# Seven products in place of eight for the output projections of two graph-attention layers, attention of two batches in one go, and a group's norms on two engines

## Chip, cores and metric

The kernel runs on one core of a Trainium2 chip. The metric is the device time of the program in microseconds, 2984.36 us before the change (median of three runs, 2982.48 to 2985.09). The engines are named as in the profile: PE is TensorE (matrix products), PEld its weight loads, DVE is VectorE, ACT is ScalarE, POOL is GpSimd, and SP issues the DMA transfers.

## What is computed

There are 128 batches of 128 nodes with 512 features, in float32, and a mask of 128 x 128 for each batch. Two layers follow each other. Each is masked attention (4 heads of 64 in layer 0, 8 in layer 1), an output projection, the sum with the layer's input, and a norm over the 512 features:

```python
q, k, v = heads(x @ Wq), heads(x @ Wk), heads(x @ Wv)
sim = einsum('bhid,bhjd->bhij', q, k) * 64 ** -0.5
attn = softmax(where(mask, sim, neg))        # layer 1: mask | eye, and it norms x with gamma, beta before q, k, v
out = einsum('bhij,bhjd->bhid', attn, v)
x = layernorm(x + merge(out) @ Wo + bo)      # Wo: 256 x 512 in layer 0, 512 x 512 in layer 1
```

## The kernel before

Two batches form a group (`G = 2`), so there are 64 groups. The loop at the end runs `step(s)` for s = 0 to 66 (lines 591 to 600), with some work of the last batches after it. One step holds work of four groups, in a pipeline: the q, k, v products of layer 0 for group s (`product_0`, line 337), scores, masks and exponentials of layer 0 for group s - 1 and of layer 1 for group s - 3 (`scores`, line 386, for one batch of each at a time), the q and k products of layer 1 for group s - 2 and its v products one step later (`product`, line 275), and attention and output of the batches between (`attend`, line 458; `residual`, line 487). The scheduling is by hand: `step` issues everything in its order (lines 531 to 589), each engine works through its own instructions in that order, and semaphores hold an instruction back until its data are there and its buffer is free.

The q, k, v products already use a scheme of seven products instead of eight for a 2 x 2 block product (Strassen's, in Winograd's form). The two batches are the halves of the rows, the two halves of the inner dimension and of the columns are the other blocks. `sums` (line 257) makes four sums of input blocks on GpSimd, and `weight_sums` four of the weights once. The products are numbered 1 to 7 and are accumulated in three PSUM banks, which `INTO` (line 272) names: `a` takes 1, then 6, 7 and 4 on top, `f` takes 5 and then 3, `c` takes 2. Between two products of one bank the result so far is read out, by ScalarE for 1, 5, 6 and 4 and by VectorE, which adds two parts, for 2, 3 and 7.

The output projection doesn't use this scheme before the change. `attend` (line 458) multiplies probabilities and values of one batch, and ScalarE copies the result to `aT` (line 474). `residual` makes 2 (layer 0) or 4 (layer 1) products of 128 x 128 weights with 512 columns for one batch in one bank (line 493). VectorE adds the layer's input with the bias (line 499), takes mean and variance (lines 501, 503), GpSimd takes the roots (lines 506 to 517), and VectorE applies the norm (line 524). `addend` (line 476) adds the bias ahead of that, for layer 1 after ScalarE has multiplied with a ratio of roots (line 483), which stands in for a second norm of the input.

Other steps that are touched: `normalised` (line 427) takes the reciprocal of the exponentials' sums on VectorE and multiplies on GpSimd (line 433); `blocks` (line 436) turns blocks of 32 x 32 on VectorE and sends them to a scratch in HBM, and `probs_arrive` fetches them back as `pT`, transposed as a whole. The layers' inputs are transposed in the same way: `turn` (line 208), `arrive` (line 226), and then on ScalarE `in_order` for layer 0 (line 235) and `finish` with gamma and beta for layer 1 (line 245).

PSUM has eight banks: five rotate (`ps_mm`, line 44), and `a`, `f` and `a0` are fixed, with `f` shared by both layers.

Of the kernel before, what the change touches and what calls it, by code (L numbers as in the profile page):

```python
# [27 lines left out]
def kernel(ctx: ExitStack, tc: tile.TileContext, x, adj, wq, wk, wv, wo, bo,  # L28
# [13 lines left out]
    four = ctx.enter_context(tc.tile_pool(name="four", bufs=4))  # L42
    dram = ctx.enter_context(tc.tile_pool(name="dram", bufs=2, space=bass.MemoryType.DRAM))
    ps_mm = ctx.enter_context(tc.tile_pool(name="ps_mm", bufs=5, space=PSUM))
# [9 lines left out]
    later, waiting = [], []  # L54
# [5 lines left out]
    def exponentials(left=0):  # L60
        while len(waiting) > left:
            waiting.pop(0)()


    X, M = {}, {}

    def load(g):
        if g >= NG:
            return
        X[g] = four.tile([P, G, E], F32, tag="x", name=f"x_{g}")  # L70
        M[g] = four.tile([P, G, N], U8, tag="m", bufs=6, name=f"m_{g}")
        nc.sync.dma_start(X[g], x[g * G:(g + 1) * G].rearrange("b n e -> n b e"))
        nc.sync.dma_start(M[g], adj[g * G:(g + 1) * G].rearrange("b i j -> i b j"))
# [8 lines left out]
    mhalf = const.tile([P, 2], F32, name="mhalf")  # L82
# [25 lines left out]

    spare = []
    for tag, n in (("qk1", 4), ("v1", 2), ("xT1", 2), ("xs1", 2)):  # L110
        rows_n = one.tile([P, n, E], F32, tag=tag, name=f"raw_{tag}")
        spare.extend(rows_n[:, i] for i in range(n))

    def load_transposed(dst, src, name, scaled=0):
        rows, cols = src.shape
        raws = []
        for r in range(rows // P):
            if not spare:
                raw = three.tile([P, cols], F32, tag="h", bufs=7, name=f"{name}_{r}")
            else:  # L120
                raw = spare.pop(0)
            nc.sync.dma_start(raw, src[r * P:(r + 1) * P, :])
            raws.append(raw)
# [36 lines left out]
    def weight_sums():  # L160
        for w, ws in ((w1qk, wsqk), (w1v, wsv)):
            for c in range(KH):
                if w is w1qk:
                    b11, b12 = w[:, c, :, 0], w[:, c, :, 1]
                    b21, b22 = w[:, KH + c, :, 0], w[:, KH + c, :, 1]
                else:
                    b11, b12 = w[:, c, 0], w[:, c, 1]
                    b21, b22 = w[:, KH + c, 0], w[:, KH + c, 1]
                t2, t3, t4 = ws[:, 0, c], ws[:, 1, c], ws[:, 2, c]
                nc.vector.tensor_sub(t3, b22, b12)  # L170
                nc.vector.tensor_sub(b12, b12, b11)
                nc.vector.tensor_sub(t2, b22, b12)
                nc.vector.tensor_sub(t4, b21, t2)

    def weight_sums_0():
        b11, b12, b21, b22 = (w0[:, c:c + KH, h].rearrange("p c t f -> p c (t f)")
                              for c in (0, KH) for h in range(2))
        t2, t3, t4 = (ws0[:, i].rearrange("p c t f -> p c (t f)") for i in range(3))
# [4 lines left out]

    weight_sums_0()
    load_transposed(w1, w_qkv, "w_qkv", scaled=INNER[1])
    setup.append(turn_gamma_beta)
    load_transposed(wo1, w_out, "w_out")
    setup.append(weight_sums)

    WO = (wo0, wo1)  # L190
    RATIO, H, XT, QK, V, QKV = {}, {}, {}, {}, {}, {}
# [14 lines left out]
    TURNED, SCR, RAW = {}, {}, {}  # L206

    def turn(l, g, b):
        if not 0 <= g < NG:
            return  # L210
        if b == 0:
            TURNED[l] = one.tile([P, 4, G * KC * 32], F32, tag=f"turned{l}", name=f"turned{l}_{g}")
        src = X[g][:, b] if l == 0 else H[g, b]
        nc.vector.transpose(TURNED[l].rearrange("p a (b c i) -> p a b c i", b=G, c=KC)[:, :, b],
                            src.rearrange("p (c a i) -> p a c i", a=4, i=32))
        if b == G - 1:
            SCR[l] = put(TURNED[l], f"scr{l}_{g}")

    def arrive(l, g):
        if not 0 <= g < NG:  # L220
            return
        RAW[l] = one.tile([P, 4, G, KC, 32], F32, tag=f"raw{l}", name=f"raw{l}_{g}")
        fetch(RAW[l].rearrange("p a b c i -> p a (b c i)"), SCR[l])

    def first_transposed():
        xT = XT[0, 0] = one.tile([P, KC, T], F32, tag="xT0", name="xT0_0")
        for b in range(G):
            pt = mm_tile(f"xt_{b}")
            for c in range(KC):
                nc.tensor.transpose(pt[:, c * N:(c + 1) * N], X[0][:, b, c * P:(c + 1) * P], ident)  # L230
# [26 lines left out]
    def sums(l, g):  # L257
        xT = XT[l, g]
        xs = one.tile([P, 4, KH, N], F32, tag=f"xs{l}", name=f"xs{l}_{g}")
        a = xT.rearrange("p (h c) (b n) -> p b h c n", h=2, b=2)  # L260
# [6 lines left out]
        XS[l, g] = xs  # L267
# [69 lines left out]
    def product_0(g, *which):  # L337
# [5 lines left out]
        for i in which:  # L343
# [10 lines left out]
            elif first:  # L354
                tag = {"a": "a0", "f": "f"}[bank]
                ACC[0, bank] = ps_st.tile([P, 512], F32, tag=tag, name=f"{bank}0_{g}")
# [11 lines left out]
            if i in (1, 5, 6):  # L368
                e = one.tile([P, 512], F32, tag=("e5_0" if i == 5 else f"e{i}"), name=f"e0_{i}_{g}")
                EV[0, i] = e[:, :3 * P]  # L370
# [8 lines left out]
    SM, SUM, PT, AT, XB = {}, {}, {}, {}, {}  # L379
# [6 lines left out]
    def scores(k):  # L386
        both = members(k)
        made = []
        for l, g, b in both:
# [11 lines left out]
            made.append(ps)  # L401
        for (l, g, b), ps in zip(both, made):
            K = HEADS[l] // 2
            mask = M[g][:, b, :]
            if l == 1:
                m1 = two.tile([P, N], U8, tag="m1", name=f"m1_{g}_{b}")
                nc.vector.tensor_tensor(m1, mask, eye, op=ALU.max)
                mask = m1
# [8 lines left out]
            SM[l, g, b], SUM[l, g, b] = sm, total  # L417
            waiting.append(lambda sm=sm, nmax=nmax, total=total, K=K: exps(sm, nmax, total, K))
        exponentials(1)

    def exps(sm, nmax, total, K):
# [14 lines left out]
    def blocks(k):  # L436
# [6 lines left out]
        t = one.tile([P, 4, sum(HEADS), 32], F32, tag="turned", name=f"turned_{k}")  # L443
        pT = one.tile([P, 4, sum(HEADS), 32], F32, tag="pT", name=f"pT_{k}")
        for l, g, b in both:
            lo, hi = slots[l]
            sm = SM.pop((l, g, b)).rearrange("p s k (q r) -> p q (s k) r", r=32)
            nc.vector.transpose(t[:, :, lo:hi, :], sm)  # L448
            PT[l, g, b] = pT[:, :, lo:hi, :]
        lo, hi = slots[both[0][0]][0], slots[both[-1][0]][1]  # L450
        t, pT = (u[:, :, lo:hi, :].rearrange("p a h i -> p a (h i)") for u in (t, pT))
        SCR["p"] = pT, put(t, f"scrp{hi - lo}_{k}")
# [5 lines left out]
    def attend(k):  # L458
        both = members(k)
        if not both:  # L460
            return
        for l, g, b in both:
            K = HEADS[l] // 2
            pT = PT.pop((l, g, b))
            pm = mm_tile(f"av{l}_{g}_{b}")

            for h in range(HEADS[l]):
                s, kk = h % 2, h // 2
                o = pm[s * D:(s + 1) * D, kk * N:(kk + 1) * N]
                v = QKV[g][:, b, kk, 2, s * D:(s + 1) * D] if l == 0 else V[1, g][:, b, h * D:(h + 1) * D]  # L470
                nc.tensor.matmul(o.rearrange("p (a r) -> p a r", r=32), v, pT[:, :, s * K + kk, :],  # L471
                                 start=True, stop=True)
            AT[l, g, b] = two.tile([P, INNER[l]], F32, tag=f"aT{l}", name=f"aT{l}_{g}_{b}")
            nc.scalar.copy(AT[l, g, b], pm[:, :INNER[l]])  # L474

    def addend(l, k):

        for _, g, b in [m for m in members(k) if m[0] == l]:
            if l == 0:
                xin = X[g][:, b, :]  # L480
            else:
                xin = H.pop((g, b))
                nc.scalar.activation(xin, xin, AF.Copy, scale=RATIO.pop((g, b)))  # L483
            nc.gpsimd.tensor_tensor(xin, xin, (bias0, bias1)[l], op=ALU.add)  # L484
            XB[l, g, b] = xin

    def residual(l, k):
        for _, g, b in [m for m in members(k) if m[0] == l]:
            aT = AT.pop((l, g, b))
            nk = INNER[l] // P  # L490
            pm = mm_tile(f"o{l}_{g}_{b}")
            for c in range(nk):
                nc.tensor.matmul(pm, aT[:, c * P:(c + 1) * P], WO[l][:, c, :],  # L493
                                 start=(c == 0), stop=(c == nk - 1))
            if l == 0:
                y = three.tile([P, E], F32, tag="h", bufs=7, name=f"h_{g}_{b}")
            else:
                y = two.tile([P, E], F32, tag="y", name=f"y_{g}_{b}")
            nc.vector.tensor_add(y, pm, XB.pop((l, g, b)))
            st = three.tile([P, nc.vector.BN_STATS_DIM], F32, tag="st", name="st")  # L500
            nc.vector.bn_stats(st, y)
            mv = three.tile([P, nc.vector.BN_AGGR_DIM], F32, tag="mv", name=f"mv{l}_{g}_{b}")
            nc.vector.bn_aggr(mv, st)
            n = 2 - l
            ve = three.tile([P, 2], F32, tag="ve", name="ve")
            nc.gpsimd.tensor_scalar_add(ve[:, 0:1], mv[:, 1:2], EPS)  # L506
            if l == 0:


                nc.gpsimd.tensor_scalar(ve[:, 1:2], mv[:, 1:2], 1.0 + EPS, EPS * EPS,  # L510
                                        op0=ALU.mult, op1=ALU.add)
            r = three.tile([P, 2], F32, tag="rstd", name="rstd")
# [117 lines left out]
```

## Time and profile before

| | us |
|---|---|
| median of three runs | 2984.36 (2982.48 to 2985.09) |
| the profiled execution | 2984.46 |
| its span, first to last instruction | 2982.7 |
| TensorE busy | 2920.0 (98%) |
| VectorE busy | 1854.0 (62%) |
| GpSimd busy | 1567.4 (53%) |
| ScalarE busy | 1334.2 (45%) |
| output products, line 493, 1536 records | 713.2 |

The profile lists for each engine how long it was busy and, in the chain of work that ended last, which engine's work the end of the program was waiting for. A matmul in float32 appears as two records. The end of a matmul in the trace is modelled, and its duration reaches into the next matmul, so the difference of two starts is the better measure of what a group of matmuls takes. For a wait, the answer names the engine and line that ended last of all that were waited for.

### The profile page before, as it was taken

What the parts mean: (1) busy time and instruction counts of PE and PEld (TensorE: products, weight loads), DVE (VectorE), ACT (ScalarE), POOL (GpSimd) and SP (SyncE); (2) the same over time, 40 slices, a digit from 0 to 9 for tenths busy, and PEclk for the clock granted to TensorE, in tenths of its full rate; (3) what the DMA queues carried; (4) which work ended last, traced back from release to release, by engine and by line L of the source; (5) the groups of instructions that cost most, each with busy time, mean ns of one, the idle gap of its engine ahead of it and who ended that gap; (6) DMA issues with size and microseconds to landing.
All of it is one profiled execution on the core that took longest, in us unless ns stands there. A gap on an engine that the chain in (4) does not pass through costs nothing.

```text
span 2982.7 us, 59421 instructions
## 1 busy us (share of the span) xinstructions
PE 2920.0 (98%) x22089; PEld 2402.9 (81%) x22089; DVE 1854.0 (62%) x3291; ACT 1334.2 (45%) x4619; POOL 1567.4 (53%) x2055
## 2 busy tenths in 40 slices
PE   6899999999999999999999999999999999999997
PEld 5788888888888888888888888888888888888865
DVE  4466666666666666666656666666666666666654
ACT  2344444444444444444544444444444444444442
POOL 2455545545545555555555555455455455455543
PEclk8999999999999999999999999999999999999999
DMA  5454544544544544544544545545445445445332
GB/s 170 123 149 129 150 141 127 161 136 124 165 135 125 165 136 127 160 134 134 156 132 140 150 131 147 146 129 153 141 126 161 137 122 168 133 125 163 118 100 89
DMA packets 249136, 414.42 MB, mean 139 GB/s; under 512 B 41608, under 2 KB 181392, under 8 KB 248848
## 3 DMA queue, kind: packets, MB, share of 16 engines
q1 hardware_dynamic: 248848, 410.62, 46.3%
q8 instruction: 175, 2.87, 0.4%
q14 instruction: 113, 0.93, 0.1%
HBM read 209.72 MB, written 200.80 MB: 138 GB/s over the span
## 4 chain that ended last, share of the span: by engine, by line
PE 96%; DVE 1%; DMA 1%; ACT 1%; issue 0%; POOL 0%; SPq 0%; POOLq 0%; DVEq 0%; ACTq 0%
PE o L493 22%; PE qka L304 15%; PE a L361 12%; PE qkf L304 8%; PE va L304 8%; PE sc L400 6%; PE av L471 6%; PE f L361 6%; PE qkc L304 4%; PE vf L304 4%; PE c L361 3%; PE vc L304 2%; ACT sm L424 1%; DMA scrp<-turned 0%; DMA pT<-scrp 0%
## 5 line engine op out<-in xcount | busy, mean ns | idle before, releaser
L424 ACT ACTIVATE sm<-sm,nmax 128x128 f32<-128x128 f32 x1536 | 595.2, 389 | 618.6 <-DVE nmax L415 604.9
L493 PE MATMUL o<-wo,aT 128*128 128x512 f32 x1536 | 713.2, 600 | 10.0 <-ACT aT L474 10.0
L506 POOL TENSOR_SCALAR ve<-mv 128x1 f32<-128x1 f32 x256 | 57.0, 223 | 1133.0 <-DVE rec L432 798.8
L493 PEld LDWEIGHTS o<-wo,aT 128*128 128x128 f32 x1536 | 278.3, 191 | 269.3 <-issue 246.8
L433 POOL TENSOR_TENSOR sm<-sm,rec 128x512 f32<-128x512 f32 (+1 forms) x256 | 397.0, 1561 | 171.9 <-DVE rec L432 171.9
L412 DVE COPY_PREDICATED sm<-m,sc 128x512 f32<-128x512 uint8 (+1 forms) x512 | 271.0, 581 | 29.1 <-POOL sm L410 7.0
L424 ACT ACTIVATION_READ_ACCUMULATOR sm<-sm,nmax 128x1 f32 x1536 | 288.0, 187 | 0.0
L448 DVE STREAM_TRANSPOSE turned<-sm 128x512 f32<-128x512 f32 (+1 forms) x256 | 246.0, 965 | 45.0 <-POOL sm L433 45.0
L304 PE MATMUL qkf<-xs,w 128*128 128x128 f32 x2048 | 249.9, 275 | 0.1
L304 PE MATMUL qka<-xs,wsqk 128*128 128x128 f32 x2048 | 249.6, 275 | 0.0
L415 DVE TENSOR_REDUCE nmax<-sm 128x4 f32<-128x512 f32 (+1 forms) x256 | 244.0, 953 | 8.8
L304 PEld LDWEIGHTS qkf<-xs,w 128*128 128x128 f32 x2048 | 239.0, 192 | 0.6 <-POOL xs L266 0.4
L304 PEld LDWEIGHTS qka<-xs,wsqk 128*128 128x128 f32 x2048 | 239.0, 192 | 0.0
L524 DVE TENSOR_SCALAR h<-h,mv,rstd 128x512 f32<-128x512 f32 x128 | 70.0, 547 | 265.0 <-POOL rstd L513 265.0
L432 DVE RECIPROCAL rec<-total 128x4 f32<-128x4 f32 (+1 forms) x256 | 44.7, 175 | 296.6 <-ACT sm L424 296.6
L266 POOL TENSOR_TENSOR xs<-xT 128x256 f32<-128x256 f32 x256 | 186.0, 727 | 34.4 <-PE w_qkvt L129 14.5
L410 POOL MEMSET sm<- 128x512 f32 (+1 forms) x256 | 181.1, 735 | 1.4 <-DVE turned L448 1.3
L330 ACT COPY ev<-va 128x256 f32<-128x256 f32 x128 | 47.6, 372 | 298.7 <-PE va L304 298.7
L513 POOL TENSOR_TENSOR rstd<-ve,mhalf 128x2 f32<-128x2 f32 (+1 forms) x256 | 165.9, 648 | 21.3
L330 ACT COPY eqk<-qka 128x512 f32<-128x512 f32 x128 | 75.1, 587 | 214.4 <-PE qka L304 214.4
L484 POOL TENSOR_TENSOR h<-h,bias 128x512 f32<-128x512 f32 x128 | 162.7, 1271 | 7.0 <-ACT h L483 6.9
L484 POOL TENSOR_TENSOR x<-x,bias 128x512 f32<-128x512 f32 x128 | 162.2, 1267 | 0.0
(122 smaller groups left out, 5825.5 us busy)
## 6 DMA issues: line engine op xcount, KB each, us to landing
scrp<-turned SPq DMA_DIRECT2D x124, 768.0 KB, 3.3
pT<-scrp SPq DMA_DIRECT2D x496, 192.0 KB, 4.0
scr<-turned SPq DMA_DIRECT2D x127, 512.0 KB, 2.7
raw<-scr SPq DMA_DIRECT2D x508, 128.0 KB, 3.0
x<-in_x_dram SPq DMA_DIRECT2D x64, 512.0 KB, 4.2
out_dram<-y SPq DMA_DIRECT2D x128, 256.0 KB, 2.0
m<-in_adj_dram SPq DMA_DIRECT2D x64, 32.0 KB, 4.0
scrp<-turned SPq DMA_DIRECT2D x4, 512.0 KB, 3.2
```

Of the source, the lines that this page charges most:

```text
L266: nc.gpsimd.tensor_tensor(o, a0, a1, op=op)
L304: nc.tensor.matmul(o, lhsT, rhs, start=first and n == 0, stop=n == len(todo) - 1, skip_group_check=True)
L361: nc.tensor.matmul(acc[:, t * P:(t + 1) * P], lhsT, rhs, start=first and n == 0, stop=n == len(todo) - 1, skip_group_check=True)
L400: nc.tensor.matmul(ps[h % 2][:, h // 2, :], q_, k_, start=True, stop=True)
L410: nc.gpsimd.memset(sm, (NEG0, NEG1)[l])
L412: nc.vector.copy_predicated(sm[:, s], mask[:, None, :].to_broadcast([P, K, N]), ps[s][:, :K, :])
L415: nc.vector.tensor_reduce(nmax, sm, AX.X, ALU.max, negate=True)
L424: nc.scalar.activation(sm[:, s, k, :], sm[:, s, k, :], AF.Exp, bias=nmax[:, s, k:k + 1], accum_out=total[:, s, k:k + 1])
L433: nc.gpsimd.tensor_tensor(sm, sm, rec[:, :, :, None].to_broadcast([P, 2, K, N]), op=ALU.mult)
L448: nc.vector.transpose(t[:, :, lo:hi, :], sm)
L484: nc.gpsimd.tensor_tensor(xin, xin, (bias0, bias1)[l], op=ALU.add)
L493: nc.tensor.matmul(pm, aT[:, c * P:(c + 1) * P], WO[l][:, c, :], start=(c == 0), stop=(c == nk - 1))
```

## The change

Group rows are kept in one tile `R[g]`, and everything from input to output works in place in it: the bias is added to both batches at once, the output products are added part by part, and the norms are applied there. Six such tiles rotate.

- `attend(s)` now works on both batches of a group, for layer 0 of group s - 2 and layer 1 of group s - 4, once per step. In layer 0 both batches share one bank and one copy.
- `out_sums` makes the four sums of the attention outputs on GpSimd, and `weight_sums_out` those of the output weights, once. `out_product` makes the seven products, each of 256 columns. VectorE adds each bank's content to its part of `R[g]` after every product.
- PSUM: four rotating banks and `a`, `f`, `a0`, `f0`. The output products of layer 0 use `a` and `f`, those of layer 1 use `a0` and `f0`.
- `stats` and `roots` keep mean and roots of both batches together. In layer 0 the norm of batch 0 is VectorE's and that of batch 1 ScalarE's; in layer 1 both are ScalarE's, and both batches are stored by one transfer.
- The diagonal is put into both masks by one instruction (`with_self`).
- Both layers' transposed inputs share one buffer on the way out (`turned_in`) and one on the way back (`raw`).
- The order in `step` is written anew, and the loop runs one step further (s = 0 to 67) with nothing after it.

```diff
-    ps_mm = ctx.enter_context(tc.tile_pool(name="ps_mm", bufs=5, space=PSUM))
+    ps_mm = ctx.enter_context(tc.tile_pool(name="ps_mm", bufs=4, space=PSUM))
...
+    def out_product(l, g, *which):
...
+        aT, so = AT[l, g], SO[l, g]
+        hk = INNER[l] // P // 2
+        w, ws = WO[l], WSO[l]
+        EH = E // 2
+        for i in which:
+            left = {1: aT[:, 0, :hk], 2: aT[:, 0, hk:], 3: so[:, 3], 4: aT[:, 1, hk:], 5: so[:, 0],
+                    6: so[:, 1], 7: so[:, 2]}[i]
+            right = {1: w[:, :hk, :EH], 2: w[:, hk:, :EH], 3: w[:, hk:, EH:], 4: ws[:, 2],
+                     5: w[:, :hk, EH:], 6: ws[:, 0], 7: ws[:, 1]}[i]
+            bank, first = INTO[i]
...
+            acc = ACC["o", bank][:, :EH]
+            for c in range(hk):
+                nc.tensor.matmul(acc, left[:, c], right[:, c], start=first and c == 0, stop=c == hk - 1,
+                                 skip_group_check=True)
+            b, h = {1: (0, 0), 2: (0, 0), 6: (0, 1), 3: (0, 1), 5: (1, 1), 7: (1, 1), 4: (1, 0)}[i]
+            part = R[g][:, b, h * EH:(h + 1) * EH]
+            nc.vector.tensor_add(part, acc, part)
...
+    def out_sums(l, g):
...
+        so = SO[l, g] = one.tile([P, 4, K // 2, N], F32, tag=("so", "xs0")[l], name=f"so{l}_{g}")
+        halves_sums(so, AT[l, g].rearrange("p b (h c) n -> p b h c n", h=2))
...
+    def norms_0(g, mv, shift, root):
+
+        nc.vector.tensor_scalar(R[g][:, 0], R[g][:, 0], mv[:, 0, 0:1], root[:, 1, 0:1],
+                                op0=ALU.subtract, op1=ALU.mult)
+        nc.scalar.activation(R[g][:, 1], R[g][:, 1], AF.Identity, bias=shift[:, 1:2],
+                             scale=root[:, 1, 1:2])
+
+    def norms_1(g, shift, root):
+        for b in range(G):
+            nc.scalar.activation(R[g][:, b], R[g][:, b], AF.Identity, bias=shift[:, b:b + 1],
+                                 scale=root[:, 0, b:b + 1])
+        nc.sync.dma_start(out[g * G:(g + 1) * G].rearrange("b n e -> n b e"), R[g])
```

The order of a step after the change (`scores` only makes the products now; `masked` is the masking and the maximum, `exps` the exponentials):

```python
        k = 2 * s
        if s:
            load(s + 1)
        made = scores(k)
        masked(made, 0)
        masked(made, 1)
        exps(0, k)
        addend(0, s - 2)
        with_self(s - 2)
        p("qk", 4, g=s - 3)
        product_0(s, 1)
        attend(s)
        exps(1, k)
        out_sums(0, s - 2)
        product_0(s, 5)
        p("", g=-1)
        product_0(s, 2)
        p("", g=-1)
        out_product(0, s - 2, 1, 5, 2)
        normalised(k)
        addend(1, s - 4)
        out_product(0, s - 2, 6)
        product_0(s, 6)
        p("", g=-1)
        blocks(k, 0)
        out_product(0, s - 2, 3, 7)
        stats(0, s - 2, 0)
        product_0(s, 3)
        out_product(0, s - 2, 4)
        stats(0, s - 2, 1)
        p("v", 1, 5, g=s - 3)
        blocks(k, 1)
        p("v", 2, g=s - 3)
        flush()
        turn(1, s - 2)
        product_0(s, 7)
        arrive(1, s - 2)
        probs_arrive(k)
        k += 1
        made = scores(k)
        masked(made, 0)
        p("v", 6, g=s - 3)
        product_0(s, 4)
        exps(0, k)
        masked(made, 1)
        exps(1, k)
        p("v", 3, g=s - 3)
        out_sums(1, s - 4)
        out_product(1, s - 4, 1, 5, 2)
        p("v", 7, g=s - 3)
        out_product(1, s - 4, 6, 3)
        p("v", 4, g=s - 3)
        normalised(k)
        turn(0, s + 1)
        finish(s - 2)
        out_product(1, s - 4, 7)
        stats(1, s - 4, 0)
        blocks(k, 0, 1)
        arrive(0, s + 1)
        probs_arrive(k)
        p("qk", 1)
        p("qk", 5)
        out_product(1, s - 4, 4)
        stats(1, s - 4, 1)
        p("qk", 2)
        p("qk", 6)
        in_order(s + 1)
        flush()
        p("qk", 3, 7)
```

## The prediction, written before the result was known

> **What bounds the kernel now.** I read the page's busy shares first, then the chain that ended last, and then the TensorE timeline of one step in the middle of the run.
>
> ```profile
> PE 2920.0 (98%) x22089; PEld 2402.9 (81%) x22089; DVE 1854.0 (62%) x3291; ACT 1334.2 (45%) x4619; POOL 1567.4 (53%) x2055
> ...
> PE 96%; DVE 1%; DMA 1%; ACT 1%; issue 0%; POOL 0%; SPq 0%; POOLq 0%; DVEq 0%; ACTq 0%
> ```
>
> TensorE never rests and carries 96% of the chain. So a step is the sum of its matmuls, and every wait that TensorE gets is paid in full. In the timeline the columns are start, duration, engine, line, operation and count. Durations overlap the next group, so I read differences of starts.
>
> ```profile
> 1546.75 3.70 PE L493 MATMUL o<-wo,aT 128*128 128x512 f32 x8
> 1550.28 1.95 PE L304 MATMUL qka<-xT,wsqk 128*128 128x128 f32 x16
> 1552.16 0.66 PE L471 MATMUL av<-pT,qkv 128*64 128x128 f32 x8
> 1552.65 1.04 PE L471 MATMUL av<-pT,v 128*64 128x128 f32 x16
> 1553.62 1.16 PE L361 MATMUL a<-xT,w 128*128 128x128 f32 x8
> 1554.62 0.61 PE L361 MATMUL a<-w,xT 128*128 128x128 f32 x4
> ...
> 1560.56 1.88 PE L493 MATMUL o<-wo,aT 128*128 128x512 f32 x4
> 1562.28 1.03 PE L304 MATMUL va<-w,xT 128*128 128x256 f32 x4
> 1563.14 1.03 PE L304 MATMUL vf<-w,xs 128*128 128x256 f32 x4
> ...
> 1591.89 3.70 PE L493 MATMUL o<-wo,aT 128*128 128x512 f32 x8
> ```
>
> The step's period is 1591.89 - 1546.75 = 45.14 us, and 64 of them are 2889 us of the 2982.7 us span. Four records of 256 columns take 0.86 us (215 ns each), four of 512 take 1.72 us (430 each). Going into `av` or out of it costs about 0.1 us: sixteen 128-column records take 1.79 us elsewhere, 1.88 ahead of `av`; eight take 0.90, but 1.00 after it.
>
> What a wait costs is seen near the end of the run, where product 4 of `va` follows closely on VectorE's read of the same bank:
>
> ```profile
> 2878.06 0.41 DVE L335 TENSOR_TENSOR v<-va,ev 128x256 f32<-128x256 f32 x1
> 2878.53 1.13 PE L304 MATMUL va<-wsv,xT 128*128 128x256 f32 x4 [0.62 <-DVE v L335]
> 2879.59 0.66 PE L471 MATMUL av<-pT,qkv 128*64 128x128 f32 x8
> ```
>
> TensorE starts 0.06 us after VectorE's end, and those four records take 1.06 us where they take 0.96 in a steady step (1572.62 to 1573.58): 0.1 us more for the restart. A reader of PSUM starts 0.20 us after the next product's start (ACT's copy of `va`, 1563.34 against 1563.14). Last, ScalarE and GpSimd ahead of the large `qk` products of the middle step:
>
> ```profile
> 1575.11 0.35 ACT L332 COPY v<-va 128x256 f32<-128x256 f32 x1
> ...
> 1576.73 2.07 ACT L252 ACTIVATE xT<-raw,gb 128x256 f32<-128x256 f32 x4
> ```
>
> ```profile
> 1575.40 3.08 POOL L433 TENSOR_TENSOR sm<-sm,rec 128x512 f32<-128x512 f32 x2
> 1578.44 1.27 POOL L484 TENSOR_TENSOR h<-h,bias 128x512 f32<-128x512 f32 x1
> 1579.67 0.73 POOL L266 TENSOR_TENSOR xs<-xT 128x256 f32<-128x256 f32 x1
> ```
>
> Here `qk` 1 starts at 1579.54, after `xT` (done 1578.80), and `qk` 5 at 1581.33, after the first sum `xs` (done 1580.40). Both are ready in time by about 0.7 to 0.9 us. That is all the slack there is.
>
> **What the Trainium skill says.** "TensorE: Matmul & The Clock Gate", section "Back-to-back issue gap", gives N/2.4 + 2.5 ns for a warm matmul of N columns: 55.8, 109 and 216 ns for 128, 256 and 512. The trace has just twice that for a record (112, 215, 430 ns), so 256 columns are as cheap per column as 512. The same page, section "What's actually happening", lets the clock fall after an idle window of about 3.4 us. The trace agrees so far that the 0.62 us wait above slowed nothing lasting, so waits under 1 us are counted as waits alone. "PSUM — Partial Sum Buffer", section "PSUM bank collisions raise a hardware error", says that a bank is guarded as a whole against a write beside a read; the `va` lines show such a wait. "SBUF — State Buffer", section "Who interferes with whom", says that a two-port `tensor_scalar` on VectorE and GpSimd block each other. The norm of `y` (line 524), which stands beside GpSimd's work, takes 892 ns on average and that of `h` 547, which fits.
>
> **The change, part by part (per step of one group).**
>
> *Output products.* Removed: 24 records of 512 columns, 3.53 + 1.72 + 3.43 + 1.72 = 10.40 us, less 0.10 in the 3.53, which is the way out of `sc` and then falls to `qk` 4: 10.30. Added: seven products of 2 records (layer 0) and seven of 4 (layer 1), 42 x 0.2157 = 9.06 us. Gain 1.24 us.
>
> *Attention in one go.* One entry into the small tiles and one exit less: 0.19 us. Product 6 of layer 0 now waits 0.13 us for ScalarE's late copy of product 1 (a step's `a` takes 0.06 + 0.07 more than the others); in the new order that copy stands ahead of the attention copies. Together the step would be 45.14 - 1.24 - 0.19 - 0.13 = 43.58 us. There are ten more places where a product waits on another engine's result. By my walk they are met in time, output product 6 of layer 0 by only 0.1 us; I give back 0.1 (bounds 0 and 1.0, at none and at a restart of 0.1 each): 43.68.
>
> *Wait 1, a bank.* The new instruction order has output product 4 of layer 0, then `v` 1, both in bank `a`, with VectorE's add between. From product 4's end: 0.20 to the add; 0.08 as the add of `product_0` 3 stands ahead of it on VectorE (557 ns); 0.41 for 256 columns (line 335: 385 to 415); 0.05 to TensorE; 0.10 restart. 0.85 us (bounds 0.7 and 1.0), covered by nothing: all of TensorE's queue is behind `v` 1.
>
> *Wait 2, the transposed input.* `finish` now stands on ScalarE behind the copy of `v` 4, and only output product 7 (0.86 us) lies between `v` 4 and `qk` 1. From the end of `v` 4: 0.20, the copy 0.25 to the next start (1575.11 to 1575.36), the first part of `xT` 0.59, 0.05: `qk` 1 starts at 1.09 instead of 0.86. Its second matmul needs the next part, 0.50 later, and with 0.10 for the restart it ends at 1.59 + 1.56 + 0.10 = 3.25.
>
> *Wait 3, GpSimd.* `qk` 5 needs `sums` of layer 1, on GpSimd behind both `normalised` products, which need a reciprocal that VectorE reaches only after the add of output product 3 of layer 1. From that product's end (0.86 before the end of `v` 4): 0.20 + 0.33 (the add's start to the next) + 0.15 reciprocal + 0.09 + 3.04 (both `sm`) + 0.73 (first sum) + 0.05 = 4.59, that is 3.73 after `v` 4. TensorE is there at 3.25. Without waits it would have been at 0.86 + 1.79 = 2.65. Waits 2 and 3 together cost 3.73 - 2.65 + 0.10 = 1.18 us (bounds 0.6, if part of it is absorbed, and 1.8). Behind it wait all other `qk` products.
>
> *Other engines.* VectorE: four adds (2.73) and three norms (2.33) go, fourteen adds of 0.41 (5.74) come: 28.7 becomes about 29.4 us of a step. ScalarE gains three norms at 0.73 (line 483's price): 20.7 to 22.8. GpSimd gains the sums of the attention outputs, four at 0.73 and four of half that width (between 0.36 and 0.73, I take 0.45), and loses about 1 us of small roots: 24.5 to 28. All stay under 65%, so none is a bound by itself; only the places above count. The norm on ScalarE lets `turn` of layer 1 and behind it the add of `product_0` 7 go on VectorE some 22.7 us into the step; `product_0` 4, which needs that bank, is due at 23.7: covered by 1 us of `v` 6. Four rotating banks instead of five: the scores need all four at once, and the last reader, the add of `v` 2, ends 1 us earlier under `product_0` 7. The mask of both batches in one instruction, and the bias of both in one (about 2.5 us, twice line 484), cost VectorE and GpSimd nothing more. Output stores go from two of 256 KB to one of 512 KB; on SP they and the scratch transfers have about 5 us before attention needs them. The next input is fetched into a buffer shared with `finish`, behind the scratch of the attention blocks on SP; its reader comes some 8 us after `finish`. The load of `x` stands behind the store on SP; its reader is 30 us off.
>
> *Sum.* 43.68 + 0.85 + 1.18 = 45.71 us, 0.57 more than now; over 64 steps 36 us. At both ends: the last group's seven products are chained through one bank, with some 0.7 us for each of three adds, sums ahead of them, and one store twice as large: I take +5 us. In the first steps attention waits for its scratch transfer once a step and later than now (`av` waited 5.65 us for `pT` at 50.18 and 4.18 at 83.08): I take -5, so nothing for both together (bounds -10 and +15). 2984.46 + 36 = 3020. The profiled execution (2984.46) is 0.1 us from the median.
>
> **Rivals.**
> 1. *The gain arrives:* all three waits hidden, 43.68 x 64 instead of 45.14 x 64: 2984 - 93 = 2891. For it: 1.5 us of TensorE work really go. Against: waits 1 to 3 stand in the instruction order itself. Chance 0.07.
> 2. *GpSimd's and ScalarE's chain is shorter than its parts* (the other side). Place: `qk` 1 and 5. Price: the 1.18 us of waits 2 and 3, summed from seven durations, of which GpSimd's are rough by the profile. The step wins once they cost under 0.6 us, which is what wait 1 leaves of the 1.46; with none of it the step is 44.53 us: 2984 - 39 = 2945. Chance 0.13. If only wait 3 goes and `qk` 1 still ends 0.6 us late, it is 45.13: no change. Chance 0.07.
> 3. *The forecast,* with a spread of 0.4 us per step, 2994 to 3046: the waits take more than the products give. Chance 0.60.
> 4. *Worse:* GpSimd's longer queue makes the roots late, so that `turn` and `product_0` 4 behind it come late as well. It decides when the roots end over 1 us later than I walked; at 0.8 us more a step it is 3071. Chance 0.13.
>
> That the change doesn't do what it says is excluded by the instruction order: fourteen products of 256 columns stand there in each step.
>
> **Numbers.** Likeliest 3020. The range reaches from 2940 (rival 2 whole) to 3065; rival 1 and most of rival 4 are left out. About 0.2% (6 us) is what a measurement can tell from no change. Faster: 0.07 + 0.13 and 0.01 of the low edge of the case without wait 3 = 0.21; same: the other 0.06 and 0.01 of the forecast's low edge = 0.07; slower 0.59 + 0.13 = 0.72.
>
> **What would show it.** Right: a period near 45.7 us; a wait of about 0.7 us of TensorE on VectorE's output add ahead of `va` 1; waits of `qka` on ScalarE's `xT` and of `qkf` on GpSimd's `xs`, together some 1.1 us in each step; output products at 0.43 and 0.86 us. Wrong: a period under 45 us, `qkf` 5 starting without a wait, or TensorE waiting steadily at places that I have not named, such as output product 6.

## The result, and the profile after it

The changed kernel takes 3049.65 us (median, 3047.68 to 3051.54). The kernel before takes 2983.64 us on the same chip, so the ratio is 1.0221 [1.0203, 1.0239]. The forecast was 3020: slower, as said, but by 66 us and not by 36.

The shares of busy time and the shares of the chain that ended last, in the kernel after the change:

```profile
PE 2904.1 (95%) x23241; PEld 2626.2 (86%) x23241; DVE 1923.6 (63%) x3683; ACT 1485.8 (49%) x4747; POOL 1743.0 (57%) x2375
...
PE 72%; DVE 11%; POOL 9%; issue 5%; DMA 2%; ACT 1%; SPq 0%; DVEq 0%; ACTq 0%; POOLq 0%
```

TensorE's work is shorter, but it carries only 72% of the chain where it carried 96%. Most of the rest is VectorE and GpSimd: TensorE now waits for them in every step. Its waits over the whole run, with the sum in us, the number of times and the longest:

```profile
PE va L308 <- DVE r L404: 38.6, 63, 0.6
...
PE a L364 <- DVE qkv L378: 21.0, 60, 4.0
...
PE a L364 <- ACT xT L245: 16.9, 2, 10.4
```

The first comes once in each step, the second in nearly every one. The step's period, between the starts of `product_0` 2 (bank `c`) in two steps, is 45.94 us (1541.46 to 1587.40) against 45.14. The timeline from 1594 us on, with the places where TensorE stands:

```profile
1594.09 0.60 PE L400 MATMUL oa<-wso,aT 128*128 128x256 f32 x2
...
1594.84 0.41 DVE L404 TENSOR_TENSOR r<-oa,r 128x256 f32<-128x256 f32 x1
...
1595.31 1.13 PE L308 MATMUL va<-w,xT 128*128 128x256 f32 x4 [0.62 <-DVE r L404]
...
1598.61 1.91 DVE L581 TENSOR_SCALAR r<-r,mv,root 128x512 f32<-128x512 f32 x1
...
1598.83 1.42 POOL L444 MEMSET sm<- 128x512 f32 x2
...
1601.79 0.52 DVE L378 TENSOR_TENSOR qkv<-a,e 128x384 f32<-128x384 f32 x1
...
1602.36 1.16 PE L364 MATMUL a<-xT,ws 128*128 128x128 f32 x8 [0.26 <-DVE qkv L378]
...
1610.63 2.90 POOL L471 TENSOR_TENSOR sm<-sm,rec 128x512 f32<-128x512 f32 x2 [7.24 <-DVE rec L470]
...
1611.18 2.08 ACT L256 ACTIVATE xT<-raw,gb 128x256 f32<-128x256 f32 x4
...
1611.83 2.32 PE L308 MATMUL qka<-xT,w 128*128 128x128 f32 x16
...
1613.49 0.73 POOL L271 TENSOR_TENSOR xs<-xT 128x256 f32<-128x256 f32 x1
```

Differences of starts give each wait its full price, since the brackets leave out the time in which the modelled end of the matmul before still runs:

- *Wait 1* (`v` 1 in bank `a`): 1595.31 - 1594.09 = 1.22 us, where the two records take 0.43. That is 0.79, and the four records behind it take 0.96 instead of 0.86: 0.89 us.
- *`product_0` 4, not foreseen*: due at 1601.93 (0.96 after the start of `v` 6 at 1600.97), it starts at 1602.36 and takes 0.10 longer: 0.53 us. It waits for VectorE's add of `product_0` 7, which stands behind `turn` and the norm, and the norm took 1.91 us.
- *Waits 2 and 3*: `qk` 1 starts at 1611.83 instead of 1611.57 (0.86 after output product 7 at 1610.71), and `qk` 5 at 1614.27 instead of 1613.36, 0.05 us after the end of the first sum `xs` (1613.49 + 0.73 = 1614.22). With the restart 1.01 us.
- *Output product 6*: 0.07 us. Everything else takes 45.94 - 2.50 = 43.44 us.

The span grew by 64.6 us. From the first scores of step 4 to those of step 64 it grew by 46.3 (2708.96 to 2755.28), ahead of them by 9.4 (145.58 to 155.00), and behind them by 8.9 (128.2 to 137.0).

### The profile page after: what moved, and what is told of

Its sections match the earlier page's. It is cut to its first block, busy times and chain, and to the rows that moved or that the text cites. A ratio compares the mean times of both kernels' runs of the same rounds, so it can differ in the third digit from the quotient of the medians.

```text
span 3047.3 us, 62928 instructions
## 1 busy us (share of the span) xinstructions
PE 2904.1 (95%) x23241; PEld 2626.2 (86%) x23241; DVE 1923.6 (63%) x3683; ACT 1485.8 (49%) x4747; POOL 1743.0 (57%) x2375
## 4 chain that ended last, share of the span: by engine, by line
PE 72%; DVE 11%; POOL 9%; issue 5%; DMA 2%; ACT 1%; SPq 0%; DVEq 0%; ACTq 0%; POOLq 0%
PE qka L308 12%; PE a L364 9%; PE oa L400 8%; PE qkf L308 8%; PE f L364 6%; PE av L517 6%; PE of L400 5%; POOL sm L471 4%; PE qkc L308 4%; DVE r L581 4%; PE sc L428 3%; PE c L364 3%; PE oc L400 3%; PE va L308 3%; PE vf L308 2%
## 5 line engine op out<-in xcount | busy, mean ns | idle before, releaser
L471 POOL TENSOR_TENSOR sm<-sm,rec 128x512 f32<-128x512 f32 (+1 forms) x256 | 370.9, 1469 | 715.1 <-DVE rec L470 715.1
L404 DVE TENSOR_TENSOR r<-oa,r 128x256 f32<-128x256 f32 x512 | 215.2, 420 | 204.3 <-PE oa L400 190.5
L538 POOL TENSOR_TENSOR r<-r,bias 128x1024 f32<-128x1024 f32 x128 | 302.0, 2359 | 8.8 <-ACT r L537 8.8
L308 PE MATMUL qkf<-xs,w 128*128 128x128 f32 x2048 | 256.9, 279 | 7.1
L271 POOL TENSOR_TENSOR so<-aT 128x128 f32<-128x128 f32 (+1 forms) x256 | 161.5, 631 | 106.3 <-ACT aT L522 106.3
L400 PE MATMUL oa<-wso,so 128*128 128x256 f32 x768 | 213.0, 386 | 4.7 <-DVE r L404 4.7
L400 PE MATMUL of<-wo,so 128*128 128x256 f32 x768 | 208.9, 381 | 4.8 <-POOL so L271 4.8
L378 DVE TENSOR_TENSOR qkv<-c,e 128x384 f32<-128x384 f32 x64 | 35.7, 558 | 262.8 <-PE c L364 260.2
L549 DVE BATCH_NORM_STATS2 st<-r 128x6 f32<-128x512 f32 x256 | 176.4, 689 | 4.4
L400 PEld LDWEIGHTS oa<-wso,so 128*128 128x128 f32 x768 | 140.8, 190 | 36.6 <-issue 19.9
```

What stands on the lines that cost most here:

```text
L271: nc.gpsimd.tensor_tensor(o, a0, a1, op=op)
L308: nc.tensor.matmul(o, lhsT, rhs, start=first and n == 0, stop=n == len(todo) - 1, skip_group_check=True)
L400: nc.tensor.matmul(acc, left[:, c], right[:, c], start=first and c == 0, stop=c == hk - 1, skip_group_check=True)
L404: nc.vector.tensor_add(part, acc, part)
L471: nc.gpsimd.tensor_tensor(sm, sm, rec[:, :, :, None].to_broadcast([P, 2, K, N]), op=ALU.mult)
L538: nc.gpsimd.tensor_tensor(R[g], R[g], (bias0, bias1)[l][:, None, :].to_broadcast([P, G, E]), op=ALU.add)
```

## The experiments

My theory before the experiments: the change takes 1.5 to 1.7 us of TensorE work out of a step, and four waits, which lie in the order in which the instructions are issued, put 2.5 us in. Then reordering alone must bring the gain back. The rival is that the new form costs more on the other engines, so that the waits only move. Periods are differences of starts in one ordinary step in the middle of the run, and each kernel is compared with runs of the kernel before on the same chip.

| kernel | median us | ratio to before, interval | period us |
|---|---|---|---|
| the change | 3049.65 | 1.0221 [1.0203, 1.0239] | 45.94 |
| finish_early | 3322.67 | 1.1135 [1.1118, 1.1151] | about 50.7 |
| rec_early | 3037.92 | 1.0183 [1.0168, 1.0198] | 45.78 |
| finish_and_rec | 3105.77 | 1.0412 [1.0394, 1.0429] | 46.75 |
| product7_early | 2980.46 | 0.9988 [0.9979, 0.9997] | 44.73 |
| norm_first | 3017.78 | 1.0115 [1.0100, 1.0130] | 45.42 |
| memset_on_vector | 3034.36 | 1.0172 [1.0158, 1.0186] | 45.56 |
| v4_earlier | 2996.29 | 1.0042 [1.0030, 1.0055] | 44.92 |
| all_waits_out | 2941.48 | 0.9857 [0.9840, 0.9873] | 44.00 |
| all_waits_out_8 | 3000.57 | 1.0058 [1.0043, 1.0073] | 45.07 |
| waits_out_norm_first | 2909.89 | 0.9748 [0.9734, 0.9761] | 43.51 |
| early_input | 3039.66 | 1.0185 [1.0171, 1.0199] | 45.94 |
| waits_out_early_input | 2905.30 | 0.9734 [0.9721, 0.9747] | 43.51 |

Not every step is ordinary. From step 4 to step 64 the mean is 45.92 us in the changed kernel, but 44.14 in all_waits_out and 43.68 in waits_out_norm_first, where 20 and 13 of the 60 steps are longer than the period in the table.

### Three tries at waits 2 and 3, and two misses: finish_early, rec_early, finish_and_rec

finish_early:

```diff
+        finish(s - 2)
         p("v", 4, g=s - 3)
         normalised(k)
         turn(0, s + 1)
-        finish(s - 2)
```

> Only `finish` is moved ahead of `v` 4, so that ScalarE makes `xT` of layer 1 before the copy of `v` 4. Theory (two chains, both of which must be short): the wait ahead of `qk` 1 (0.26 us and a restart in each step) goes, but `qk` 5 still waits for GpSimd's first sum, which stands behind both `sm` products; it starts at the same time, so the total stays within 8 us of the changed kernel (3050). Rival (ScalarE's late `xT` is the cause and GpSimd only follows it): 30 to 60 us faster.

rec_early:

```diff
+        normalised(k)
         out_product(1, s - 4, 6, 3)
         p("v", 4, g=s - 3)
-        normalised(k)
```

> Only `normalised` is moved ahead of output products 6 and 3 of layer 1, so that VectorE takes the reciprocal about 0.9 us earlier and GpSimd's `sm` products and sums follow. Theory (two chains): the sums now wait for `xT` instead, which is as late as before; `qk` 5 starts at most 0.1 us earlier, 0 to 10 us faster than 3050. Rival (the reciprocal alone is the cause): about 0.9 us in each step, 55 us faster.

finish_and_rec has `normalised` ahead of output products 6 and 3, and `finish` between them and `v` 4:

> Both moves together. Theory (two chains): `xT` is ready before `qk` 1 and the first sum when `qk` 1 ends; both waits and their restarts go, 1.0 us in each step, 62 us faster: about 2988. Rival (the time is GpSimd's or VectorE's total load and comes back at another place): less than 20 us faster.

finish_early came out 273 us slower than the change, against the theory and the rival. The timeline of the kernel finish_early ahead of `qk` 1:

```profile
1551.18 1.03 PE L308 MATMUL va<-wsv,xT 128*128 128x256 f32 x4
...
1552.24 2.08 ACT L256 ACTIVATE xT<-raw,gb 128x256 f32<-128x256 f32 x4 [1.39 <-PE va L308]
...
1554.23 0.35 ACT L336 COPY v<-va 128x256 f32<-128x256 f32 x1
...
1554.63 2.05 PE L308 MATMUL qka<-xT,w 128*128 128x128 f32 x16 [1.56 <-ACT v L336]
```

I had treated `finish` as free to move up, but it overwrites `xT`, of which there is one buffer, and `v` 4 is the last to read it. So ScalarE waits for `v` 4 (1.39 us), then makes the whole of `xT` (2.08), and only then copies `v` 4 out of bank `a`, which `qk` 1 needs. By the starts, `qk` 1 is 1.73 us late (1554.63 instead of 1552.90), where it was 0.26 late; `qk` 5 is then in time, so this fault costs 0.8 us of a step. Placed ahead of `normalised`, `finish` also puts its sums ahead of the `sm` products on GpSimd, and GpSimd then waits for `xT`, 618 us in the whole run. What GpSimd does after that comes late as well, the memsets of the score tiles among it, so that VectorE masks late (it waits 377 us for the memsets, 83 in the changed kernel) and TensorE waits for the masking ahead of attention:

```profile
PE av L517 <- DVE sm L446: 137.4, 60, 3.0
```

That is still not all of it. In steps 5 to 62 this wait is 1.8 to 3.0 us long. In 16 of these 58 steps the attention products behind it take 2.77 us at a granted clock of 1.00, as in the changed kernel; in the other 42 the clock is 0.50 to 0.67 while they run, and they take 4.06 to 5.32 us. What goes beyond 2.77 us adds up to 67 us. finish_and_rec lacks this second fault and has the first: its period is 0.81 longer, and it is 56 us slower than the change instead of 62 faster. A second buffer for `xT` was not tried.

rec_early gained 12 us, close to the 0 to 10 of the theory. GpSimd's `sm` products now end in time, but the wait for `qk` 5 stays:

```profile
1607.98 0.73 POOL L271 TENSOR_TENSOR xs<-xT 128x256 f32<-128x256 f32 x1 [1.53 <-ACT xT L256]
```

GpSimd now waits 1.53 us for the last part of `xT` on ScalarE. So wait 3 had two causes in a row: taking away GpSimd's own uncovers ScalarE's, and waits 2 and 3 have to be taken away together.

### v4_earlier: both causes at once

```diff
-        out_product(1, s - 4, 1, 5, 2)
         p("v", 7, g=s - 3)
-        out_product(1, s - 4, 6, 3)
+        out_product(1, s - 4, 1, 5, 2)
         p("v", 4, g=s - 3)
         normalised(k)
-        turn(0, s + 1)
+        out_product(1, s - 4, 6, 3)
         finish(s - 2)
+        turn(0, s + 1)
```

> `v` 7 goes ahead of output products 1, 5, 2 of layer 1, `v` 4 and `normalised` ahead of 6 and 3, and `finish` stays behind the copy of `v` 4. Theory (`finish` can't overwrite `xT` before `v` 4 has read it, so `v` 4 itself must come earlier): `finish` starts right behind the exponentials, 1.5 us earlier than now; waits at `qk` 1 and `qk` 5 and their restarts go, 1.0 us in each step: about 2988. Rival (GpSimd can't have the first sum earlier whatever the order is, since its queue is full): `qk` 5 still waits 0.5 us or more, 3020 or slower.

Here `v` 4 itself comes up, with its copy, `normalised` and `finish` behind it, and three output products cover them. TensorE's timeline in the kernel v4_earlier:

```profile
1579.31 1.03 PE L400 MATMUL oa<-wso,so 128*128 128x256 f32 x4
1580.18 1.95 PE L308 MATMUL qka<-xT,w 128*128 128x128 f32 x16
...
1581.96 1.95 PE L308 MATMUL qkf<-xs,w 128*128 128x128 f32 x16
```

`qk` 1 starts 0.87 us after output product 7, and `qk` 5 1.78 us after `qk` 1: neither waits. The period falls by 1.02, the price that the trace gave for both waits (1.01). The profiled execution took 2986.89 us, as expected. The other executions spread more than those of other kernels (to 3001.70), and the median, 2996, is 8 us above the 2988 of the theory; why is open.

### product7_early, norm_first and memset_on_vector: wait 1 and `product_0` 4

product7_early puts another product between output product 4 and `v` 1, and gives the add of `product_0` 7 more time:

```diff
         out_product(0, s - 2, 4)
         stats(0, s - 2, 1)
+        product_0(s, 7)
         p("v", 1, 5, g=s - 3)
...
         turn(1, s - 2)
-        product_0(s, 7)
```

> Only `product_0` 7 is moved up, between output product 4 of layer 0 and `v` 1. Theory (a bank that is read between two neighbours): TensorE has 1.34 us of other work while VectorE reads bank `a`, so the wait ahead of `va` 1 (0.79 and a restart) goes; the add of `product_0` 7 is then done before the slow norm on VectorE, so the wait ahead of `product_0` 4 (0.43 and a restart) goes as well: 1.4 us in each step, 88 us faster, 2962; up to 0.15 us may come back where the scores now follow the add of `v` 2 closely. Rival (TensorE has only run ahead of the others there and will wait for them at another place): less than 30 us faster.

Both waits went: output product 4 starts at 1558.71 and `product_0` 7 follows 0.43 later, `v` 1 without a gap. The period fell by 1.21, not by the 1.42 that the two waits cost: the layer-1 part of the second scores takes 1.19 us (1563.72 to 1564.91) where it takes 0.99 in the changed kernel. So the gain is 69 us and not 88, far from the rival's 30. This edit alone makes the change as fast as the kernel before (0.9988).

The next two tell why the norm took 1.91 us. norm_first moves it away in time:

```diff
-        p("v", 2, g=s - 3)
         flush()
+        p("v", 2, g=s - 3)
```

> Only the two norms of layer 0 are moved ahead of `v` 2, so that VectorE's norm can start when the roots are there (about 0.7 us earlier) and before GpSimd begins to clear the score tiles. Theory (the two engines block each other): the norm on VectorE (line 581) takes 0.55 to 0.9 us instead of 1.9, the add of `product_0` 7 ends before `product_0` 4 is due, and the wait of 0.43 us with its restart goes: about 30 us faster than 3050. Rival (the norm is slow by itself, by its per-partition operands in place): it still takes 1.9 us; it starts 0.7 us earlier, so the wait shrinks to under 0.1, but line 581 shows no change.

memset_on_vector leaves the norm where it is and moves GpSimd's memset instead:

```diff
-            nc.gpsimd.memset(sm, (NEG0, NEG1)[l])
+            nc.vector.memset(sm, (NEG0, NEG1)[l])
```

> The changed kernel with the memsets of sm (line 444) moved from GpSimd to VectorE, where they stand right ahead of the masks and behind the norm; nothing else is moved. Theory, that the norm of layer 0 on VectorE takes 1.91 us because GpSimd's memset runs at the same time: the norm takes 0.55 us at its old place, and the wait at product_0 4 (0.53 us) goes, so turn is 1.4 us earlier. The masks come some 0.5 us later by the memset's own time on VectorE, which may lengthen the wait for qk 5, so the time is only bounded: 3010 to 3050 us. Rival, that the norm is slow for what VectorE reads and writes there, or that GpSimd's next work (the sums of the attention outputs, which then start earlier) blocks it as well: 1.2 us or more.

The line of the norm (smallest, median and largest duration in ns), first of the changed kernel, then of norm_first, then of memset_on_vector:

```profile
L581 DVE TENSOR_SCALAR r<-r,mv,root x64: 535/1911/1916, 89.8 to 2968.9; 128x512 f32<-128x512 f32 x64
```

```profile
L581 DVE TENSOR_SCALAR r<-r,mv,root x64: 545/546/548, 88.1 to 2936.8; 128x512 f32<-128x512 f32 x64
```

```profile
L581 DVE TENSOR_SCALAR r<-r,mv,root x64: 543/547/1087, 87.7 to 2953.8; 128x512 f32<-128x512 f32 x64
```

So the same instruction takes 0.55 us or 1.91 us, and GpSimd's memset beside it makes the difference; the roots, which feed it, were not late. The Trainium skill, "SBUF — State Buffer", section "Who interferes with whom", says that a two-port operation on VectorE and GpSimd share ports, and that one of them is then blocked entirely. These runs agree that one is held back; they don't show by which ports. In both kernels the wait at `product_0` 4 is gone. norm_first gained 31.9 us (0.53 x 60 = 32). memset_on_vector gained 15.3: its period is 0.38 shorter, not 0.53, since `v` 7 and output product 6 of layer 1 take 0.94 us each instead of 0.86, and 8 of the 60 steps take 0.35 more.

The changed kernel shows the same without any edit. The smallest value of its line, 535, stands for a few steps in which the norm is short, such as this one:

```profile
497.18 0.54 DVE L581 TENSOR_SCALAR r<-r,mv,root 128x512 f32<-128x512 f32 x1
497.71 1.41 POOL L444 MEMSET sm<- 128x512 f32 x2
```

Here the memset begins as the norm ends, and the norm isn't held back. Three of the 60 steps between step 4 and step 64 are like that, and they take 45.41 us, 0.53 less than the others.

### all_waits_out, waits_out_norm_first, all_waits_out_8: the change with its waits taken out

all_waits_out has the edits of v4_earlier and product7_early, and one more for the second scores:

```diff
+        p("v", 6, g=s - 3)
         k += 1
         made = scores(k)
         masked(made, 0)
-        p("v", 6, g=s - 3)
```

> The order of the run before, `product_0` 7 between output product 4 of layer 0 and `v` 1, and `v` 6 ahead of the second scores (so that these don't stand directly behind the add of `v` 2). Theory: nothing is left of the four waits; the period is 43.4 to 43.7 us against 45.14 in the kernel before, and the total 2900 to 2915. Rival (some other wait takes their place as soon as TensorE is faster, GpSimd being busy for 27 of 43.5 us): over 2935.

It beat the kernel before by 1.4%, but 2941 us is in the rival's range and not in the theory's: a new wait had come, at output product 7 of layer 1. The timeline of all_waits_out there:

```profile
1596.32 1.03 PE L400 MATMUL oa<-wso,so 128*128 128x256 f32 x4
...
1597.81 0.20 DVE L470 RECIPROCAL rec<-total 128x8 f32<-128x8 f32 x1 [1.59 <-ACT sm L462]
...
1597.93 0.37 DVE L404 TENSOR_TENSOR r<-oa,r 128x256 f32<-128x256 f32 x1
...
1598.45 1.10 PE L400 MATMUL oa<-wso,so 128*128 128x256 f32 x4 [0.25 <-DVE r L404]
```

Product 6 starts at 1596.32 and its add could run at about 1597.4 (0.86 for the product, 0.20 to the read). But on VectorE the reciprocal of layer 1 stands ahead, and waits 1.59 us for the last exponential. Product 7, of the same bank, starts at 1598.45 instead of 1598.04. I suspected the norm, still 1.45 us long here, of pushing masks and exponentials back, and added the edit of norm_first:

> The kernel of all_waits_out, with the norms of layer 0 (the call of flush in the middle of the step) moved ahead of product 2 of v. Theory, that the wait at output product 7 of layer 1 (0.25 us, 0.41 with the restart) is left over from VectorE's norm, which takes 1.45 us there beside GpSimd's memset and pushes the masks, the exponentials and so the reciprocal of layer 1 back until it stands ahead of the add of output product 6: VectorE's norm at 0.55 us, no wait at output product 7 of layer 1, period 43.5 to 43.7 us instead of 44.00, 2915 to 2927 us. Rival, that the reciprocal comes late because ScalarE's exponentials are late for reasons of their own: the norm gets short, the wait at output product 7 stays, 2935 to 2945 us.

In the kernel waits_out_norm_first the reciprocal waits 0.30 us, and product 7 follows in time:

```profile
1577.51 1.03 PE L400 MATMUL oa<-wso,so 128*128 128x256 f32 x4
1577.66 0.20 DVE L470 RECIPROCAL rec<-total 128x8 f32<-128x8 f32 x1 [0.30 <-ACT sm L462]
...
1579.24 1.03 PE L400 MATMUL oa<-wso,so 128*128 128x256 f32 x4
```

The step takes 43.51 us, 0.07 from the 43.44 of the change without its waits. The trace marks no wait of TensorE in this step; of the 13 longer ones, 10 have a wait of 0.4 to 0.9 us of attention for VectorE's masking. The time is 2909.89 us, below the expected 2915: 2.5% faster than before and 4.6% faster than the change as it was. So order, not load, made the change slow.

all_waits_out_8 keeps the order of all_waits_out, but makes the eight block products themselves (`hk` blocks of the right side taken from the weights in the same way, `nc_` is `2 * hk` for product 4), each added by VectorE, without GpSimd's sums of the attention outputs:

```diff
-            left = {1: aT[:, 0, :hk], 2: aT[:, 0, hk:], 3: so[:, 3], 4: aT[:, 1, hk:], 5: so[:, 0],
-                    6: so[:, 1], 7: so[:, 2]}[i]
+            left = {1: aT[:, 0, :hk], 2: aT[:, 0, hk:], 3: aT[:, 0, hk:], 4: aT[:, 1], 5: aT[:, 1, :hk],
+                    6: aT[:, 0, :hk], 7: aT[:, 1, hk:]}[i]
...
-                nc.tensor.matmul(acc, left[:, c], right[:, c], start=first and c == 0, stop=c == hk - 1,
+                nc.tensor.matmul(acc, left[:, c], right[:, c], start=c == 0, stop=c == nc_ - 1,
...
     def out_sums(l, g):
+        return
```

> The same order, but the output projection without the scheme of seven: eight block products (the fourth place has two), each placed where the seven were and in the same banks, no sums of the attention outputs on GpSimd and none of the output weights. Theory (the scheme is worth its 7 to 8 and its sums cost nothing): 6 more records of 256 columns a step, 1.29 us, 80 us slower than the run before, so about the time of the kernel before (2983 to 2995). Rival (the sums on GpSimd, 4.8 us a step, hold others up): less than 50 us slower.

It is 59 us slower than all_waits_out, between the theory's 80 and the rival's 50: 1.07 us per step against 1.29 of matmuls (two more records in layer 0, four in layer 1). Most of the 0.2 us between them stands at output product 7 of layer 1, where both kernels still wait, all_waits_out for 0.49 us with the restart and all_waits_out_8 for 0.33. So in this order the seven products are worth what TensorE saves less 0.2 us, even though GpSimd is busy for 306 us more with them (1746.6 against 1440.7). In the order of waits_out_norm_first the eight products were not run.

### early_input and waits_out_early_input: the start

Both have the same edit, early_input on the changed kernel and waits_out_early_input on waits_out_norm_first:

```diff
+        if s < 2:
+            turn(0, s + 1)
+            arrive(0, s + 1)
         out_product(0, s - 2, 1, 5, 2)
...
+        if s > 1:
             turn(0, s + 1)
...
+        if s > 1:
             arrive(0, s + 1)
```

> The changed kernel with the early input of waits_out_early_input alone. Theory, that the start costs the change 9 us of its 65 because of the two waits for xT of groups 1 and 2 (16.9 us together): 3034 to 3042 us, the period still 45.94 us. Rival, that the start is set by the weights: 3046 to 3050 us.

> The kernel of waits_out_norm_first, and in steps 0 and 1 alone the turned input of the next group is written and fetched back before the output products of layer 0 instead of at the end of the step, where TensorE, having little work yet, catches up with the fetch. Theory, that the two waits for the copies of xT of groups 1 and 2 (together 19 us in all_waits_out) are what the kernel with seven output products pays at its start: most of them go, 8 to 16 us less than waits_out_norm_first. Rival, that these waits only stand in for the loading and turning of the weights, which the same steps carry: the time moves to other waits in the first 150 us, less than 4 us gained.

TensorE's waits in the first 160 us, first of the changed kernel, then of early_input:

```profile
PE a L364 <- ACT xT L245: 16.9, 2, 10.4
```

```profile
PE c L364 <- DVE sm L446: 8.1, 1, 8.1
...
PE av L517 <- DMA pT<-scrp: 4.5, 1, 4.5
PE a L364 <- ACT xT L245: 1.9, 1, 1.9
```

The 16.9 us went down to 1.9, but 8.1 and 4.5 came in their place. The first scores of step 4 come at 151.02 us instead of 155.00. So this edit wins 4 us at the start and not 9. The median's gain of 10 is within what the theory gave, but partly by luck: 5.5 us of it lie between step 4 and step 64, where 13 steps instead of 3 take 45.41 us, those in which the norm is short (0.54 to 1.02 us). In waits_out_early_input the gain is 4.6 us in all, and the scores of step 4 come 2.5 us earlier (148.03 against 150.56). That lies between the theory and its rival: the input was one limit of the start, with others close behind. At 2905.30 us this is the fastest kernel of the study.

## Why the prediction was right on the sign and short on the size

- *Output products and base step.* The products take 0.43 and 0.86 us as priced, and the step without waits 43.44 where I walked 43.58. Right.
- *Wait 1.* Forecast 0.85, measured 0.89, in the place named. Right.
- *Waits 2 and 3.* Forecast 1.18 together, measured 1.01, in the places named and by the mechanism named; v4_earlier took 1.02 away. Right, and rivals 1 and 2 fall with it. What I had not seen is that ScalarE's `xT` stands right behind GpSimd's chain as the next limit (rec_early).
- *The step that failed: "`product_0` 4, which needs that bank, is due at 23.7: covered by 1 us of `v` 6".* The cover holds only with a short norm: with 0.55 us, the add that ends at 1602.31 would have ended at 1600.95, 0.98 ahead of 1601.93. GpSimd's memset beside the norm makes it 1.91 us, 1.36 more than alone, which uses up the 1 us and costs 0.53 us. I had quoted the contention for two lines of the kernel before, and did not ask what GpSimd does while the one norm left on VectorE runs. norm_first and memset_on_vector show it. Rival 4 had the place and a price of that order (0.8), but not the cause: it blamed late roots.
- *Output product 6.* I gave back 0.1; it costs 0.07.
- *The other mis-sized term: the two ends, "nothing for both together (bounds -10 and +15)".* Measured +18. At the start I counted that attention would no longer wait for `pT`: right (11.2 us in three waits before, none after). But the input of groups 1 and 2, fetched back at the end of a step, is then late (16.9 us), and so is `xT` of layer 1 in the first steps (6.9 us of waits where there was 1.1). At the end, the chain through one bank and the sums ahead of it come as foreseen, but the end costs 8.9 us where +5 was taken. TensorE's waits behind step 64, first before, then after:

```profile
PE av L471 <- DMA pT<-scrp: 7.5, 2, 4.9
PE o L493 <- ACT aT L474: 7.4, 5, 2.5
```

```profile
PE av L517 <- DMA pT<-scrp: 7.6, 1, 7.6
PE oa L400 <- DVE r L404: 6.5, 7, 2.0
PE of L400 <- POOL so L271: 4.8, 2, 3.0
```

The waits for bank `a` and for the sums, 11.3 us, stand where 7.4 us of waits for the copy stood; all of TensorE's waits there grew by 3.1 us. In the last 46 us the granted clock is 0.75, against 0.90 in the last 46 us before. No run took the end alone apart, so how the 8.9 us divide between waits, clock and the one step more is open.

In figures: the period is 0.80 us longer instead of 0.57 (+0.53 and +0.04, less 0.17, 0.14 and 0.03), and what counts is 60 steps between the ends, not 64. Those give 46.3 us where the forecast had 36 for all, and the ends give 18 where it had none. The total came nearer than the account behind it: 0.34 us of each step that were priced too high hide more than half of the 0.53 that was missed.

## What to carry to other kernels

When TensorE is the bound and its work gets shorter, walk every place where a product waits for a bank or an operand, with the durations that the instructions have beside their new neighbours, and not alone. Before moving a step up, ask which reader its output buffer waits for: one order cost 273 us because a single buffer tied `finish` to the last product of the group before, and GpSimd's queue stood behind `finish`. When a wait is taken away, the next cause behind it may be only tenths of a microsecond off; the gain came whole only once all of them were moved, and the change went from 2.2% slower to 2.7% faster without any change to what is computed.

## What the runs showed of the hardware that was not expected

- A memset on GpSimd, which reads nothing, stretched VectorE's `tensor_scalar` from 0.55 to 1.91 us. The norm's record begins at 1598.61, 0.22 us ahead of the memset's, and still ends 0.27 us behind the memset's end (1600.25). In the short case (497.18) the norm begins just as far, 0.09 us, ahead of GpSimd's instruction before the memset (line 574, at 1598.70 and at 497.27), but there it is line 574 that is stretched, from 0.20 to 0.50 us. So the starts in the record don't tell which of the two gives way.
- A matmul group that restarts after a wait for a semaphore took about 0.10 us more in the steps shown here (0.96 for 0.86, 0.99 for 0.89, 1.89 for 1.79), whether the start was 0.43 us late or 1.73.
- A wait of 1.8 to 3.0 us ahead of attention in finish_early was followed by a granted clock of 0.50 to 0.67 in 42 of 58 steps, and by 1.00 in 16. The waits of up to 0.91 us in the changed kernel and of 1.7 us in finish_and_rec, once in each step, left it at 1.00 (1500 to 1600 us). The idle window of about 3.4 us that the prediction quotes is thus not a bound below which a wait costs only itself.
